# A two-layer attention kernel: pair sums formed behind the transposes, and half of an image's transposes kept in DRAM

## The chip, the cores and the metric

The kernel runs on one core of a Trainium2 chip. The time is device microseconds of one execution; the median of five runs before the change is 2765.83 us (2765.57 to 2766.76). Engines are named as the profile names them: PE (TensorE), DVE (VectorE), ACT (ScalarE), POOL (GpSimd), SP (SyncE, which only issues DMAs here). PEld is the loading of weights into PE.

## The reference, cut to what matters

The input x is 8 images of 256 channels and 96 x 96 pixels, float32. Two residual layers follow each other:

```python
x = x + layer0(group_norm(x))   # q, k, v = 1x1 convolutions, fft2 of each over (h, w)
                                # attention among the 32 channels of each of 8 heads
                                # out = abs(ifft2(attn @ v_f, axes=(-2, -1))) while out is (head, 32, 9216)
                                # then an output convolution
x = x + layer1(group_norm(x))   # linear attention with softplus features, 32 key channels
```

Layer 0 normalizes each row of the transformed q and k over all 9216 frequencies and takes softmax of the real and of the imaginary part of q k^T. The kernel computes no transform as such. q k^T over all frequencies needs only the covariance of x with x (for the norms) and of x with its mirrored image (pixel (h, w) beside pixel (-h, -w), modulo 96). With e = x + mirrored x and o = x - mirrored x both follow from e e^T and o o^T over half of the pixels; a pixel that is its own mirror gets the weight 1/sqrt(2). The inverse transform runs over the 32 channels and over the 9216 frequencies as one axis, so it does not undo the forward one: what is left of the two over the pixels is that each row of the image is multiplied by a 96 x 96 matrix that depends on the row (a window of a table). The code calls this rotating.

## The kernel before, in words

Channels lie on partitions: an image is [128, 2, 9216]. Two arenas in SBUF hold an image each; x of image b is in one, its rotated form y in the other, where x of image b+1 is loaded as soon as regions become free. Inside an arena the rows are permuted: tile t of 12 holds rows 4t to 4t+3 and then their mirrored rows (x_col, L102; tile 0 also holds rows 0 and 48). Tiles are worked from 11 down to 0.

For each image there are these stages, written as generators that yield between small pieces:

- `pair_sums(b)` (L323): 37 steps, 3 for each tile and one for the row that is left. `even_odd` (L296) makes e and o of a whole tile with one addition and one subtraction (L317; on Pool for most tiles, on VectorE for some, and a narrow column by Pool at L318), one tile or two ahead of their use. A step transposes a block of 128 pixels of e and of o on PE (L350, four transposes into one PSUM tile), ACT copies the result to a slot of `xT` (L353), and PE adds the products e e^T and o o^T (L331, eight matmuls; each float32 matmul appears as two in the profile). The products of a step are written after the transposes of the next one. VectorE takes the statistics of x for the group norm (L264).
- `attention(b)` (L367): group norm, then a chain of small matmuls and VectorE and ACT work that ends in the matrix `mz`.
- `rotate(b)` (L525): 48 steps of two rows. A step transposes two rows of x (L550, four transposes of 128 x 96), ACT copies them to a slot of `xT` (L563), and two steps later PE multiplies them with the row's window of the table (L553, eight matmuls in the profile), and VectorE copies the result into y (L558 for a column of sums, L559 for the pixels, backwards). `load_r` (L533) loads the windows of six rows into one of three `tm` buffers, from ACT's DMA queue (from SP's for image 0) in pieces of 384 bytes, and Pool fills one more column (L536).
- `images(b)` (L582): z = mz y (L621), squares and roots on ACT with additions on VectorE (L662) and Pool (L667), the output convolution (L633), the residual sum and the statistics for layer 1. x of image b+1 begins to be loaded.
- `layer1(b)` (L680): group norm, q and k (L718), softplus on VectorE and ACT, transposes of x (L779) copied out by ACT or VectorE (L782, L784), the products with k (L755).
- `output(b)` (L835): matmuls (L863), residual sums on VectorE (L868) and on Pool after an ACT copy (L871, L872), stores. The last tiles of x of image b+1 are loaded here.

The order of the work: `weave(stage, other)` (L884) runs a stage, and at each yield of n it takes n steps of the other one. `pair_sums(b + 1)` is woven into images, layer1 and output of image b; its last six steps follow alone (`finish`, L915). `rotate(b)` is woven into `attention(b)`; its last steps follow alone (L907). In attention the program's order holds on PE, in output on PE, DVE, Pool and SP; elsewhere a scheduler that plans with a cost model orders the instructions of each engine. [...] Buffers come from pools: `ring` has four buffers (e and o of a tile, the tiles of images, weights, scratch), `three` has three (`tm`), `psum` five banks.

## Time and profile before

| what | us |
|---|---|
| median of 5 runs | 2765.83 |
| the profiled execution | 2764.56 |
| its span, first to last instruction | 2762.7 |
| PE busy | 2720.2 |
| DVE busy | 1958.5 |
| ACT busy | 1367.6 |
| POOL busy | 843.5 |
| one image, from the last product of pair_sums to the same point of the next (412.82 to 752.64) | 339.8 |
| of it rotate with attention (412.8 to 490.6) | 77.8 |
| of it images (491 to 626), layer1 (626 to 680) and output with the last six steps (680 to 753) | 135, 54, 73 |
| transposes of rotate (L550), 1520 of them, busy on PE | 409.2 |
| matmuls of rotate (L553), 3040 of them, busy on PE | 472.7 |
| sums on Pool (L317), 136 of 128 x 760 | 246.0 |

In what follows a row of a group of instructions reads: line, engine, operation, output and input by name and shape, count, then busy time, mean nanoseconds of one, and the idle time of that engine ahead of them with what ended it. A row of the timeline reads: start, duration, engine, line, operation, count, and in brackets the idle time of the engine ahead of it with what ended it. A row of the waits reads: engine and line, what it waited for, total, times, longest. PE's instructions overlap, so that busy times of PE do not add up to elapsed time; the step from one instruction's start to the next does.

### The profile page before, as it was taken

Reading aid. Unit: us, or ns where it says so; the run is one execution under the profiler, and the core shown is the slowest. Engines: PE = TensorE matmul, PEld = TensorE weight load, DVE = VectorE, ACT = ScalarE, POOL = GpSimd, SP = SyncE. Lnnn points to the kernel's source line nnn. Section 1 sums busy time; section 2 is a strip of 40 time slices with the busy share of each in tenths; the row PEclk is TensorE's granted clock in tenths of the full one; section 3 lists DMA queues with packets and bytes.
Section 4 is the critical chain, followed back from the end, with each engine's and each line's share of the span. In section 5 each row is a group of like instructions: output and inputs, shape, how many; then the busy total and the mean of one; then the engine's idle time right before and its main releaser. Section 6 shows DMA issues by size and latency. Waiting matters only on the chain.

```text
span 2762.7 us, 47785 instructions
## 1 busy us (share of the span) xinstructions
PE 2720.2 (98%) x18348; PEld 1972.2 (71%) x18348; DVE 1958.5 (71%) x4104; ACT 1367.6 (50%) x2098; POOL 843.5 (31%) x939
## 2 busy tenths in 40 slices
PE   8999999999999999999999999999999999999988
PEld 8965679657795677956679567785678856788556
DVE  7588666876668767587675875769766687666776
ACT  3455634556345563354634546345453455544553
POOL 5034340342403423035230351313513135131311
PEclk9999999999999999999999999999999999999997
DMA  5120151201512015120151201521015210251003
GB/s 169 40 69 8 47 184 43 70 7 49 179 43 72 6 47 182 43 69 6 54 178 46 63 6 54 182 54 52 7 53 184 57 46 7 64 176 29 0 7 137
DMA packets 197273, 192.50 MB, mean 70 GB/s; under 512 B 88820, under 2 KB 197048, under 8 KB 197048
## 3 DMA queue, kind: packets, MB, share of 16 engines
q1 hardware_dynamic: 129800, 164.34, 18.5%
q10 hardware_dynamic: 67248, 25.12, 3.5%
q8 instruction: 146, 2.39, 0.4%
q14 instruction: 79, 0.65, 0.1%
HBM read 113.85 MB, written 75.57 MB: 69 GB/s over the span
## 4 chain that ended last, share of the span: by engine, by line
PE 93%; DVE 3%; ACT 2%; DMA 1%; issue 1%; POOL 1%; SPq 0%; POOLq 0%; DVEq 0%; ACTq 0%
PE z L621 20%; PE po L633 18%; PE acc L331 12%; PE y L553 10%; PE xr L550 6%; PE xT L779 5%; PE eoT L350 5%; PE kq L718 5%; PE o L863 4%; PE kx L755 3%; DMA arena<-in_x_dram 1%; PE cw L423 1%; PE kT L770 1%; DVE arena L559 1%; PE mz L511 1%
## 5 line engine op out<-in xcount | busy, mean ns | idle before, releaser
L621 PE MATMUL z<-arena,mz 128*128 128x384 f32 (+2 forms) x2400 | 595.0, 476 | 0.0
L633 PE MATMUL po<-e,wo 128*128 128x384 f32 x1536 | 529.7, 486 | 0.2 <-ACT e L668 0.2
L667 POOL TENSOR_TENSOR e<-e 128x768 f32<-128x768 f32 x192 | 348.1, 1815 | 554.1 <-ACT e L666 554.1
L621 PEld LDWEIGHTS z<-arena,mz 128*128 128x128 f32 (+1 forms) x2400 | 325.6, 163 | 241.4 <-issue 42.4
L553 PE MATMUL y<-tm,xT 96*128 96x97 f32 x3040 | 472.7, 261 | 1.7 <-ACT sd_a L288 0.5
L553 PEld LDWEIGHTS y<-tm,xT 96*128 96x128 f32 x3040 | 457.8, 192 | 12.5 <-issue 4.9
L331 PE MATMUL acc<-xT 128*128 128x256 f32 (+2 forms) x2368 | 439.8, 327 | 3.5 <-ACT xT L353 3.5
L633 PEld LDWEIGHTS po<-e,wo 128*128 128x128 f32 x1536 | 289.4, 190 | 197.7 <-DVE arena L635 1.2
L662 DVE TENSOR_TENSOR e<-z,xT 128x768 f32<-128x768 f32 x384 | 365.9, 953 | 85.2 <-PE z L621 85.1
L264 DVE BATCH_NORM_STATS2 st<-arena 128x6 f32<-128x384 f32 x768 | 406.7, 553 | 11.1 <-DMA arena<-in_x_dram 0.8
L550 PE MATMUL xr<-ident,arena 128*96 128x128 f32 x1520 | 409.2, 275 | 0.0
L331 PEld LDWEIGHTS acc<-xT 128*128 128x128 f32 (+1 forms) x2368 | 379.6, 191 | 37.6 <-ACT xT L353 5.2
L563 ACT COPY xT<-xr 96x512 f32<-96x512 f32 (+1 forms) x384 | 220.6, 578 | 293.5 <-PE xr L550 289.0
L666 ACT ACTIVATE e<-e 128x1536 f32<-128x1536 f32 x192 | 284.5, 1482 | 93.3 <-DVE e L662 91.8
L668 ACT ACTIVATE e<-e 128x768 f32<-128x768 f32 x192 | 162.0, 844 | 334.0 <-POOL e L667 332.9
L317 POOL TENSOR_TENSOR eo<-arena 128x760 f32<-128x760 f32 x136 | 246.0, 1809 | 252.3 <-issue 129.9
L635 DVE TENSOR_TENSOR arena<-arena,po 128x384 f32<-128x384 f32 x384 | 211.3, 552 | 94.4 <-PE po L633 70.5
L353 ACT ACTIVATE xT<-eoT 128x512 f32<-128x512 f32 x280 | 166.8, 598 | 183.2 <-PE eoT L350 181.6
L550 PEld LDWEIGHTS xr<-ident,arena 128*96 128x96 f32 x1520 | 227.2, 150 | 10.3 <-issue 6.9
L559 DVE COPY arena<-y 128x384 f32<-128x384 f32 (+1 forms) x384 | 209.9, 547 | 1.2 <-issue 0.5
L558 DVE COPY ys<-y 128x4 f32<-128x4 f32 (+1 forms) x384 | 62.5, 163 | 199.1 <-PE y L553 195.7
L350 PE MATMUL eoT<-ident,eo 128*128 128x128 f32 (+1 forms) x1184 | 189.0, 280 | 11.8 <-POOL eo L318 11.8
(202 smaller groups left out, 2912.6 us busy)
## 6 DMA issues: line engine op xcount, KB each, us to landing
arena<-in_x_dram SPq DMA_DIRECT2D x184, 384.0 KB
out_dram<-arena SPq DMA_DIRECT2D x184, 384.0 KB
tm<-rt ACTq DMA_DIRECT2D x112, 216.0 KB
tm<-rt SPq DMA_DIRECT2D x16, 216.0 KB
arena<-in_x_dram SPq DMA_DIRECT2D x8, 288.0 KB
out_dram<-arena SPq DMA_DIRECT2D x8, 288.0 KB
wl<-in_w1t_dram SPq DMA_DIRECT2D x8, 256.0 KB
wl<-in_w2t_dram SPq DMA_DIRECT2D x8, 256.0 KB
```

Of the source, the lines that this page charges most:

```text
L264: nc.vector.bn_stats(out=st[:, k, c, :], in_=x_of(b)[:, k, c * CH:(c + 1) * CH])
L317: op(d[:, :, lo:hi, 1:W], x_t[:, :, ra:ra + n, 1:W], x_t[:, :, back, W - 1:0:-1])
L331: mm = nc.tensor.matmul(acc[c][:, m * C:m * C + (KC - m) * P], lhsT=t[0:np_, c, m * P:(m + 1) * P], rhs=t[0:np_, c, m * P:C], start=(first ...
L350: nc.tensor.transpose(pt[0:np_, c * C + k * P:c * C + (k + 1) * P], eo[:, c, k, i:i + np_], ident)
L550: nc.tensor.transpose(pt[0:W, r * C + k * P:r * C + (k + 1) * P], x_of(b)[:, k, o:o + W], ident)
L553: nc.tensor.matmul(pu[:, o:o + W + 1], lhsT=gt[0:W, r, k * P:(k + 1) * P], rhs=tm[:, g % TR + r, :], start=True, stop=True)
L559: nc.vector.tensor_copy(y[:, :, :, g + r:g + 2], src[:, :, W - 1::-1, r:2])
L621: mm = nc.tensor.matmul(out[:, o:o + n * W], lhsT=columns(mz, k, c, j), rhs=y[:, k, h * W:(h + n) * W], start=(k == 0 and o == 0), stop=(k ...
L633: nc.tensor.matmul(po[:, 0:CH], lhsT=wo[:, k, m * P:(m + 1) * P], rhs=e[:, k, :], start=(k == 0), stop=(k == KC - 1))
L662: nc.vector.tensor_add(e[:, 2 * c:2 * c + 2, :].rearrange("p t (q h) -> p t q h", h=H), pz[:, 0:CH].rearrange("p (q h) -> p q h", h=H).uns ...
L666: nc.scalar.activation(e, e, AF.Square)
L667: nc.gpsimd.tensor_add(e[:, 0:2, :], e[:, 0:2, :], e[:, 2:4, :])
```

## The change

1. **e and o are made after the transposes.** `even_odd` goes. A step of `pair_sums` now transposes a block of x itself and a mirrored copy of its partners (`back`, two buffers), again four transposes into one PSUM tile. ACT copies both to SBUF with a weight for each pixel (`pw`, a column for each kind of step: 0 for a pixel that would count twice, 1/sqrt(2) for one that is its own mirror), and then e and o are formed of the two in a slot of `xT`: by Pool from SBUF (two operations of 256 columns), or by VectorE from PSUM and SBUF. In later images Pool does it for tiles 9 to 11 and for all but the first step of tiles 0 to 5, VectorE for the rest; in image 0 they alternate. The mirrored copy is made one step ahead by Pool, by ACT for tiles 0 to 5 of later images. Column 0 of the image goes through a small tile `w0`, filled by Pool; the last two steps of an image, which mix pieces of rows 0, 48 and `w0`, need 8 and 9 small copies.
2. **Half of the transposes are kept in DRAM.** In images 1 to 7 the steps of tiles 6 to 11 also store the transposed x and the transposed mirrored copy to `xtd` in DRAM (two DMAs of 128 KB a step from SP), and two transposes of `w0` supply column 0. In `rotate` the rows 24 to 71 except 48 and 49 are then loaded from there three steps ahead (`fetch`, 192 KB for a step, SP), in place of four transposes and an ACT copy. Rows that come from the mirrored copy are stored the other way round, so their table windows come from a second table `rb`.
3. **The order of rotate** alternates between three steps of one kind and three of the other (`pieces`). The windows of the table are put together once, stored to `rx` in DRAM and read back from there as one block by later images; all these DMAs are issued from SP.
4. **Smaller shifts.** Three yields in attention become longer (3, 5, 3 to 4, 8, 4); the weights `wl` are loaded at the second step of tile 0 instead of at the start of attention; two buffers for layer 1 are taken at the start of images; in layer 1 half of VectorE's copies of transposed x go to ACT.

The diff, cut to its core:

```diff
+        def turn_back(i):
+            t, j = steps[i]
...
+            front = ab[0][2] if ready else xts[-1][:, j % 3, 0].rearrange("p (k n) -> p k n", k=KC)
+            for p0, n, *v in ab:
+                for c in range(ready, 2):
+                    if v[c] is not None:
+                        (nc.scalar.copy if b and t < T0 else nc.gpsimd.tensor_copy)(
+                            (front, back[:, i % 2])[c][:, :, p0:p0 + n], v[c])
+            return front, xts[-1][:, j % 3]
...
+        for i, (t, j) in enumerate(steps):
+            front, both = ahead
+            if i + 1 < len(steps):
+                ahead = turn_back(i + 1)
+            pt = ps_tile(f"eoT_{b}_{t}_{j}").rearrange("p (c n) -> p c n", c=2)
+            for k in range(KC):
+                nc.tensor.transpose(pt[:, 0, k * P:(k + 1) * P], front[:, k], ident)
+                nc.tensor.transpose(pt[:, 1, k * P:(k + 1) * P], back[:, i % 2, k], ident)
+            nc.scalar.activation(both, pt, AF.Copy, scale=pw[:, j:j + 1])
+            if b and t >= T0:
+                n = P - j // 2
                 for c in range(2):
...
+                    nc.sync.dma_start(out=turned(c, PR * t, 1 + P * j)[0:n], in_=both[0:n, c])
+            eo = sum_slot()[:, :, 0:C]
+            if (j if t < T0 else t > NT - 4) if b else j % 2:
+                nc.gpsimd.tensor_add(eo[:, 0], both[:, 0], both[:, 1])
+                nc.gpsimd.tensor_sub(eo[:, 1], both[:, 0], both[:, 1])
+            else:
+                for c, op in enumerate((ALU.add, ALU.subtract)):
+                    nc.vector.scalar_tensor_tensor(eo[:, c], in0=pt[:, 0], scalar=pw[:, j:j + 1], in1=both[:, 1],
+                                                   op0=ALU.mult, op1=op)
+            if pending is not None:
+                products(*pending, first, False)
...
-        yield 3
+        yield 4
...
-            yield (5, 3)[m]
+            yield (8, 4)[m]
...
+            turned = H // 2 <= h < H - PR * T0
+            if b > turned:
+                nc.sync.dma_start(out=tm, in_=rx[h // TR])
+                return tm
...
+        pieces = [TR * i for i in (15, 4, 0, 5, 14, 6, 1, 8, 13, 7, 2, 9, 12, 10, 3, 11)]
+        order = [h + r for h in pieces for r in range(0, TR, 2)]
...
+        def fetch(i):
+            if i < len(order) and spilled(order[i]):
+                xts[i] = xT[:, i % NX]
+                h = order[i]
+                c = h > H // 2
+                rows = turned(c, H - h - 1 if c else h, 0)[0:2 * W]
+                nc.sync.dma_start(out=xts[i][0:W, :, 0:C], in_=rows.rearrange("(r w) n -> w r n", w=W))
...
+            step(None if spilled(h) else h, pending.pop(0) if len(pending) == 2 else None, xts[i])
+            pending.append((h, xts.pop(i), tm))
+            fetch(i + 3)
...
-                    if jj or i % 3 == 2:
+                    if jj or i % 6 > 1:
                         nc.scalar.copy(xt[jj][:, :, 0:C], src)
```

## The prediction

> **What bounds the kernel.** I read the page first, busy time and then the chain that ended last; after it the waits of PE alone, and the timeline wherever the change touches the order of work.

> ```profile
> PE 2720.2 (98%) x18348; PEld 1972.2 (71%) x18348; DVE 1958.5 (71%) x4104; ACT 1367.6 (50%) x2098; POOL 843.5 (31%) x939
> PE 93%; DVE 3%; ACT 2%; DMA 1%; issue 1%; POOL 1%; SPq 0%; POOLq 0%; DVEq 0%; ACTq 0%
> PE z L621 20%; PE po L633 18%; PE acc L331 12%; PE y L553 10%; PE xr L550 6%; PE xT L779 5%; PE eoT L350 5%; PE kq L718 5%; PE o L863 4%; PE kx L755 3%; DMA arena<-in_x_dram 1%; PE cw L423 1%; PE kT L770 1%; DVE arena L559 1%; PE mz L511 1%
> ```

> PE is on the chain for 93% of the span, in every stage. A busy PE need not be a fast one, so I asked what PE itself ever waits for:

> ```profile
> PE eoT L350 <- POOL eo L318: 11.8, 21, 7.0
> PE kT L770 <- DVE arena L748: 3.6, 1, 3.6
> PE acc L331 <- ACT xT L353: 3.5, 7, 0.5
> ```

> The whole list comes to about 32 us in 2762.7 (columns: total, times, longest). So PE work that is taken away shortens the span, and every wait that is added to PE lengthens it.

> **What goes.** Of the 48 steps of rotate in an image, the pairs of rows from 24 to 70 except 48 lose their four transposes (L550): 23 steps in each of images 1 to 7, 161 steps, 644 of 1520 transposes. The price of one step is in the trace, since the last steps of rotate already run without transposes. The start of the small copy (L558) marks the steps:

> ```profile
> 823.08 0.16 DVE L558 COPY ys<-y 128x4 f32<-128x4 f32 x1 [0.61 <-PE y L553]
> ...
> 824.31 0.17 DVE L558 COPY ys<-y 128x4 f32<-128x4 f32 x1 [0.61 <-PE y L553]
> ...
> 827.67 0.16 DVE L558 COPY ys<-y 128x4 f32<-128x4 f32 x1 [0.27 <-PE y L553]
> ...
> 828.57 0.17 DVE L558 COPY ys<-y 128x4 f32<-128x4 f32 x1 [0.27 <-PE y L553]
> ```

> A mixed step takes 1.235 us (821.84 to 824.31 is two), a step without transposes 0.895 us (826.78 to 828.57 is two), and VectorE still waits 0.27 us for PE in it. Saved: 161 x 0.34 = 55 us. The chain of waits puts a transpose at 0.11 us, which would make 161 x 0.44 = 71 us; but those two steps are free of gaps on PE and nevertheless take 0.11 us for each of 8 matmuls, against 0.10 us for each of the 12 in the mixed step, so I take 55. The small end: VectorE has 0.71 us of copies in a step (L558 and L559) and is busy for 11.26 of the 15 us from 445 to 460, where the softmax lies. If some 8 spilled steps of an image gain nothing there, 7 x 8 x 0.34 = 19 us are lost and 36 remain.

> [...]

> **What is added to PE directly.** Two small transposes of w0 in each later image: 14 x 0.11 = +1.5 us. The 37 x 4 transposes and 37 x 8 products of pair_sums stay as many.

> **The new path of a sum.** Before, Pool or VectorE had made e and o a whole tile ahead, and a product waited for ACT alone. Now it waits for transposes, then ACT, then the sum:

> ```profile
> 743.57 0.60 ACT L353 ACTIVATE xT<-eoT 128x512 f32<-128x512 f32 x1 [1.15 <-PE eoT L350]
> ...
> 744.95 1.39 PEld L331 LDWEIGHTS acc<-xT 128*128 128x128 f32 x8
> ...
> 745.42 1.42 DVE L317 TENSOR_TENSOR eo<-arena 128x570 f32<-128x570 f32 x2 [0.80 <-DMA arena<-in_x_dram]
> ```

> ACT ended at 744.17, its products start at 744.95: 0.78 us of slack for c=0, and 0.65 us more (four of the eight products, 1.31 us) for c=1. ACT now takes a scale per partition: the form with half takes 689 ns, not 598, so 0.69 us of slack remain. A sum of 256 columns on Pool lies between L318 (8 columns, 0.21 us when undisturbed) and L872 (384 columns, 1.004 us); with L667 (768, 1.815 us) the slope is 2.1 ns a column, so 0.735 us. On VectorE L830 (256 columns, one operand in PSUM) takes 0.381 us. So a VectorE step is covered; a Pool step is late by 0.05 us for c=0 and, with 0.735 us more, 0.1 us for c=1 plus semaphores. In output PE has 0.98 us of o matmuls in each step besides, and in the kq stage 5.3 us: covered. Uncovered are three places.

> (a) The six steps after output. Pool and SP keep the program's order there. The copies for (0,0), among them four w0 copies on Pool, are written ahead of the sum of (1,2), and all need the last tile of x, which lands at 745.42 (the row above, VectorE waiting for it). ACT's order is the scheduler's. Then come 8 and 9 small copies on ACT for the last two steps. Their bounds are L726 (1 column, 0.203 us) and L405 (128 columns, 0.263 us), so about 0.23 us each, 4 us together, against 1.75 us of PE (0.44 + 1.31) a step and 0.69 us of ACT. Followed through by hand the last product ends about 2 us later than now, less if ACT puts its ready work first: 1.5 us an image, +10.5 us, ends 0 and 3.5 us an image (0 and +24).

> (b) Around layer1's group norm three steps stand almost alone on PE (629 to 635). Pool then makes for each step two sums, a mirrored copy (L224, 48 columns, 0.218 us, and L530, 192 columns, 0.524 us, give 0.66 us for 256) and a third of the w0 copies: 1.47 + 0.66 + 0.22 = 2.35 us against 1.75. That is 0.6 us x 3 if nothing was made ahead: +1 us an image, +7 us, ends 0 and +14.

> (c) In the kx stage (645 to 680) ACT is busy for 27.08 of 35 us and gets 6 copies more (L782, 0.59 us) and 0.09 us per step: 31.4 of 35. I take +0.5 us an image, +3.5 us, ends 0 and +7.

> The trace shows Pool held up by VectorE: at 734.30 two L318 took 1.80 us while two L317 ran, elsewhere 0.21 us each. [...]

> [...]

> **Waits whose cover shrinks.** In the attention the matmul of qkm (L392) waits for the reciprocal of the deviation:

> ```profile
> 759.44 0.15 DVE L379 TENSOR_TENSOR dmm<-mv_a,rstd_a 128x2 f32<-128x2 f32 x1
> ...
> 759.72 0.53 PEld L392 LDWEIGHTS qkm<-wl,dmm 128*2 128x2 f32 x8
> ```

> The slack is 0.13 us. The two steps ahead of it become spilled ones, shorter by 0.68 us: +0.55 us, +3.9 us for seven images. Elsewhere the longer yields (4, 8, 4 for 3, 5, 3) give as much cover as before: 8 steps of about 1.05 us against 5 of 1.235.

> The spilled loads: ACT's 23 copies (L563) go, a load of 192 KB comes in their place, issued after step i for a step whose matmuls run five steps later, at least 4.4 us. The nearest row is the load of tmat, 0.73 to 4.15 us, 3.4 us with the start of the program in it: hidden with 1 us to spare. SP took 0.47 us to issue a quiet weight load (L371), under 0.89. The tm loads move from ACT's queue to SP behind the out stores, which land by 750.95 (Pool's L530 waits for them); the first tm is needed at 756.4. The 36 large stores an image (128 KB each) fall into 626 to 680, where the DMA share is 0.19 at most, not into 715 to 753, where it is 0.87 to 0.91. All at nothing.

> **Image 0** has no spill. Its sums on VectorE stand in order behind tables(), about 6 us of VectorE work (L233 to L253) that an e and o made ahead used to hide; on the other side the first step needs a 0.66 us copy where PE waited 7.0 us for Pool. Ends -3 and +6, I take +2.5.

> **Sum**, against the profiled execution's 2764.56 us (span 2762.7): -55 + 1.5 + 10.5 + 7 + 3.5 + 3.9 + 2.5 = -26.6. The median is 1.3 us above the profiled time: 2765.8 - 26.6 = 2739.

> **Rivals.** *Cover holds everywhere*: -55 + 1.5 = 2712. For it speaks that the waits in (a) to (c) are each under 4 us and ACT is at 50%; against it the slack of 0.05 us. Chance 0.15. *The sums become the path*: if a product waits for both sums, a Pool step needs 0.09 + 0.69 + 1.47 + 0.1 = 2.35 us against 1.75, 0.6 us late in 8 steps of each later image and 13 of image 0 (41 us), with 14 us for the small copies: -55 + 1.5 + 3.9 + 41 + 14 + 3.5 + 2.5 = +11, 2777. It turns the sign once a later image loses 7.1 us ((55 - 1.5 - 3.9) / 7). Against it: the products of c=0 come first. Chance 0.13. *Spilled steps stay as long*: if a load costs SP what it does in output, where 16 issues took 19.65 us (1.23 us each), a spilled step stays near 1.235: no saving, +25, 2791. Against it the DMA share of 0.16 in rotate. Chance 0.05. *The costs eat the gain*, at the upper ends of (a) to (c) and image 0: -55 + 1.5 + 24 + 14 + 7 + 3.9 + 6 = +1, 2767. Chance 0.10. The forecast keeps 0.57.

> **Numbers.** A measurement of this kernel tells 0.2% (5.5 us) from no change. Faster: 0.57 + 0.15 = 0.72; within: 0.10; slower: 0.13 + 0.05 = 0.18. The forecast's own range is 2714 to 2760; the one given, 2706 to 2772, takes in full cover and the eaten gain, and leaves out most of the 0.18 and a little below.

> **What would show it.** L550's successor with 876 transposes and 14 for w0; spilled steps 0.89 us apart by the small copy; PE's waits naming Pool's sums only around group norm and after output, under 4 us an image. Wrong if products wait for Pool or VectorE in most steps, if y waits for a DMA, or if the spilled steps are paced by VectorE.

## The result, and the profile after

The changed kernel takes 2772.23 us (median of 22 runs, 2764.69 to 2784.29), the kernel before on the same chips 2765.74 (41 runs): a ratio of 1.0025, interval 1.0018 to 1.0031. The change costs 0.25%, where the forecast was a gain of 27 us. The profiled execution took 2775.92 us with a span of 2774.1. It is 11.4 us longer than the span before; the medians differ by 6.5 us. The times now scatter by 20 us where they scattered by 10, and this execution lies in the upper half; why they scatter is a part of the answer.

The page's first line and the waits of PE (total, times, longest), to be read beside those of before:

```profile
PE 2693.2 (97%) x17718; PEld 1941.8 (70%) x17718; DVE 1967.7 (71%) x4237; ACT 1372.5 (49%) x2230; POOL 848.9 (31%) x1199
```

```profile
PE acc L329 <- POOL xT L406: 22.6, 24, 3.3
PE acc L329 <- DVE xT L410: 11.0, 7, 1.6
PE qkm L459 <- issue: 7.7, 7, 1.1
PE eoT L398 <- POOL back L383: 4.7, 3, 2.2
PE eoT L397 <- DMA arena<-in_x_dram: 4.6, 1, 4.6
```

PE is busy for 27 us less (2693.2 for 2720.2), and waits in three places where it did not: products for Pool's sums, products for VectorE's sums, once an image, and qkm (the last two rows belong to image 0). The chain of waits is no help here: it can be followed only through the last 70 us.

The spilled steps are what the forecast said, 0.89 to 0.90 us apart (VectorE's timeline, start and duration; before 1.235):

```profile
767.80 0.16 DVE L657 COPY ys<-y 128x4 f32<-128x4 f32 x1 [0.35 <-PE y L652]
767.88 0.55 DVE L658 COPY arena<-y 128x384 f32<-128x384 f32 x1
768.70 0.17 DVE L657 COPY ys<-y 128x4 f32<-128x4 f32 x1 [0.27 <-PE y L652]
```

So I cut both traces at the same instructions and compared stage by stage. "Tail" is from the end of the last o product to the last product of the sums, and "rotate" from there to the first matmul of the next stage; us, summed over the seven times that each occurs.

| stage | before | after | difference |
|---|---|---|---|
| image 0, start to last product | 74.7 | 80.8 | +6.1 |
| rotate of images 1 to 7 | 514.7 | 476.7 | -38.0 |
| images 0 to 6 | 1021.7 | 1022.0 | +0.3 |
| layer1, images 0 to 6 | 513.4 | 529.7 | +16.3 |
| output, images 0 to 6 | 229.9 | 225.5 | -4.4 |
| tails | 101.3 | 131.3 | +30.0 |
| last image behind its rotate | | | +1.1 |

Two rows hold what was not foreseen. A tail takes 17.3 to 19.9 us (before 14.1 to 14.8). And rotate takes 66.7 or 66.8 us in four images, 6.8 less than before, but 69.9 or 70.0 in three. The windows of the trace say why (stretch; busy us of PE, PEld, DVE, ACT, POOL with counts; granted clock, DMA share, GB/s):

```profile
1089.90:1093.30 3.40, 1.16 (x6) 1.09 (x7) 0.00 (x0) 1.85 (x7) 1.92 (x6) 1.00 1.05 363
1093.30:1096.70 3.40, 3.40 (x14) 2.92 (x13) 1.03 (x3) 2.58 (x11) 1.93 (x3) 0.51 0.71 234
...
1106.90:1110.40 3.50, 2.40 (x23) 2.21 (x23) 2.52 (x11) 2.13 (x3) 0.00 (x0) 1.00 0.10 16
1110.40:1113.80 3.40, 3.40 (x17) 2.13 (x14) 1.17 (x4) 0.00 (x0) 0.00 (x0) 0.50 0.18 54
1113.80:1117.20 3.40, 3.40 (x19) 3.40 (x19) 3.06 (x10) 0.64 (x2) 0.00 (x0) 0.50 0.21 61
```

A stretch of 3.4 us in which PE stood idle for 2.2 us (the tail) or 1.1 us (ahead of qkm) is followed by one or two stretches at half the granted clock. There are 11 halved stretches between images 1 and 7, five in tails and six in rotate, and none before the change. Half speed for 3.41 us loses up to 1.7 us: up to 8.5 us in the tails, and 3 x 3.2 = 9.7 us in rotate (69.9 against 66.7).

### The profile page after: what moved, and what is told of

It is laid out like the page before. It is cut to its first block, busy times and chain, and to the rows that moved or that the text cites. A ratio compares the mean times of both kernels' runs of the same rounds, so it can differ in the third digit from the quotient of the medians.

```text
span 2774.1 us, 47811 instructions
## 1 busy us (share of the span) xinstructions
PE 2693.2 (97%) x17718; PEld 1941.8 (70%) x17718; DVE 1967.7 (71%) x4237; ACT 1372.5 (49%) x2230; POOL 848.9 (31%) x1199
## 5 line engine op out<-in xcount | busy, mean ns | idle before, releaser
L740 PE MATMUL po<-e,wo 128*128 128x384 f32 x1536 | 529.7, 486 | 0.2 <-ACT e L775 0.2
L329 PE MATMUL acc<-xT 128*128 128x256 f32 (+1 forms) x2368 | 454.7, 334 | 33.6 <-POOL xT L406 22.6
L329 PEld LDWEIGHTS acc<-xT 128*128 128x128 f32 x2368 | 386.7, 193 | 80.3 <-POOL xT L406 27.9
L652 PE MATMUL y<-tm,xT 96*128 96x97 f32 x3040 | 430.4, 270 | 4.9 <-ACT xT L661 3.6
L652 PEld LDWEIGHTS y<-tm,xT 96*128 96x128 f32 x3040 | 419.2, 195 | 16.7 <-issue 8.5
L399 ACT ACTIVATE xt<-eoT,pw 128x512 f32<-128x512 f32 x296 | 202.6, 687 | 165.2 <-PE eoT L398 161.5
L661 ACT COPY xT<-xr 96x512 f32<-96x512 f32 (+1 forms) x223 | 127.3, 575 | 281.1 <-PE xr L649 281.1
L649 PE MATMUL xr<-ident,arena 128*96 128x128 f32 x876 | 231.5, 278 | 0.0
L410 DVE SCALAR_TENSOR_TENSOR xT<-eoT,pw,xt 128x256 f32<-128x256 f32 x258 | 112.2, 477 | 114.1 <-ACT xt L399 98.5
L971 DVE TENSOR_TENSOR arena<-arena,o 128x384 f32<-128x384 f32 x288 | 142.1, 550 | 35.9 <-PE o L966 35.7
L383 POOL COPY back<-arena 128x256 f32<-128x256 f32 (+1 forms) x167 | 72.6, 441 | 302.9 <-PE eoT L398 302.7
```

What stands on the lines that cost most here:

```text
L329: mm = nc.tensor.matmul(acc[c][:, m * C:m * C + (KC - m) * P], lhsT=t[0:np_, c, m * P:(m + 1) * P], rhs=t[0:np_, c, m * P:C], start=(first ...
L399: nc.scalar.activation(both, pt, AF.Copy, scale=pw[:, j:j + 1])
L649: nc.tensor.transpose(pt[0:W, r * C + k * P:r * C + (k + 1) * P], x_of(b)[:, k, o:o + W], ident)
L652: nc.tensor.matmul(pu[:, o:o + W + 1], lhsT=gt[0:W, 1 - r if back else r, k * P:(k + 1) * P], rhs=tm[:, g % TR + r, :], start=True, stop=True)
L740: nc.tensor.matmul(po[:, 0:CH], lhsT=wo[:, k, m * P:(m + 1) * P], rhs=e[:, k, :], start=(k == 0), stop=(k == KC - 1))
```

## Theories

- **O, order.** In the tail, copies that need the last tile of x stand in ACT's and Pool's queues ahead of work that is due. PE runs dry, and the idle PE then gets half the clock.
- **D, transfers.** The added DMAs make x's last tile land later.
- **S, thin stream.** Rotate now feeds PE so thinly that its clock is halved, whatever the waits do.

For O speaks the timeline of a tail of the changed kernel:

```profile
1088.59 0.27 PE L398 MATMUL eoT<-ident,back 128*128 128x128 f32 x1
1090.38 0.24 ACT L383 COPY xt<-arena 128x64 f32<-128x64 f32 x1 [3.99 <-DMA arena<-in_x_dram]
...
1090.53 0.68 ACT L399 ACTIVATE xt<-eoT,pw 128x512 f32<-128x512 f32 x1
...
1091.36 0.72 POOL L406 TENSOR_TENSOR xT<-xt 128x256 f32<-128x256 f32 x1 [4.82 <-ACT xt L399]
...
1092.14 1.85 PE L329 MATMUL acc<-xT 128*128 128x256 f32 x8 [3.27 <-POOL xT L406]
```

PE finished the transposes of step (1,1) at 1088.86. ACT could have taken them then; but a copy of 64 columns for step (0,2), four steps later, stands ahead of it and waits for x until 1090.38. ACT, Pool's sum and PE's product follow in a row.

## The experiments

All are compared with the kernel before; the ratio is given with its interval.

### One cause each

**e1_tail**: ACT too keeps the program's order in output, and the copies for (0,0) are written behind the sum of (1,2).

```diff
+            late = b and (t, j) == (1, 2)
-            if i + 1 < len(steps):
+            if i + 1 < len(steps) and not late:
...
+            if late:
+                ahead = turn_back(i + 1)
...
-        with tc.manual_schedule(engines={mybir.EngineType.PE, mybir.EngineType.DVE, mybir.EngineType.Pool, mybir.EngineType.SP}):
+        with tc.manual_schedule(engines={mybir.EngineType.PE, mybir.EngineType.DVE, mybir.EngineType.Pool, mybir.EngineType.SP,
+                                         mybir.EngineType.Activation}):
```

> Edit to the changed kernel: in output ACT too keeps the program's order, and the copies for the first step of tile 0 are written after the activation and the sum of the step before. Theory O (order): in the changed kernel a copy out of the last tile of x stands ahead of the activation of step (1,1) in ACT's queue, PE idles 1.7 to 3.3 us for it, and where that idle fills much of a 3.4 us stretch the granted clock is halved in the next one. Then the wait of the products for Pool in the last six steps falls under 0.5 us, the time from the last matmul of output to the last product from 17.4 to 19.9 us down to about 15, the five halved stretches in these places go, those in rotate (after the wait of qkm) stay: 7 x 2.5 + 5 x 1.7 = 26 us less, about 2746. Rival D (DMA): the last tile of x lands too late because of the added DMA traffic, the order does not matter: the wait moves to the transposes of (0,0) and the time stays at 2772. Rival S (thin stream): the clock is halved because rotate keeps PE less dense: the same ten or so halved stretches, about 2755.

Measured: 2755.9 us, 0.997 (0.9958 to 0.9982). The tails fall from 131.3 to 117.6 us. That is less than O expected, because two new waits came with the same order: 16 small copies now stand in a row ahead of the activations of the last two steps, and Pool's copy of a column of y waits 3.1 us for an output store ahead of a sum. The time is the one S named, but not for its reason: rotate takes 66.7 or 66.8 us in six of seven images, with its stream as thin as ever.

**e2_yield3**: one more step of rotate ahead of qkm, to cover VectorE's chain.

```diff
-        yield 2
+        yield 3
         pb = ps_tile(f"qkm_{b}")
```

> Edit to the changed kernel: one more step of rotate ahead of the matmul of qkm (yield 3 for 2). Theory O: PE's 1.1 us wait there goes (7.7 us in all), and with it the three pairs of halved stretches early in rotate, 3 x 3.3 us; rotate takes 66 us in each of images 1 to 7; the tail stays as it is: about 17 us less, 2755. Rival S (the clock is halved because rotate without half of its transposes is a thinner stream): only the 7.7 us go, the halved stretches in rotate stay, 2764. Rival D expects what O does here.

Measured: 2756.11 us, 0.9971 (0.9962 to 0.998). Rotate takes 65.9 or 66.0 us in six images and 66.7 in one, with no halved stretch in it. O holds, S does not: the stream of those steps is the same. The tails stay at 129.3 us.

**e4_fill**: 24 transposes of the identity into a spare bank, ahead of the product that waits in the tail.

```diff
+            if b and (t, j) == (1, 2):
+                idle = ps_tile(f"idle_{b}")
+                for k in range(24):
+                    nc.tensor.transpose(idle[:, k % 4 * P:(k % 4 + 1) * P], ident, ident)
```

> Edit to the changed kernel: 24 transposes of the identity that nothing reads are put on PE after the transposes of step (1,2) of images 1 to 7, 24 x 0.11 = 2.6 us, where PE idles 1.7 to 3.3 us now. Theory O: the wait is filled, not shortened, so that the halved stretches of the tail go (5 x 1.7 = 8.5 us) while 2.6 us stand in place of 1.7 or 3.3 of idle: between 2762 and 2770, and the clock record shows halved stretches in rotate alone. Rival S, and any theory in which idle time of PE is not what halves the clock: as many halved stretches as before, and 2774 to 2778.

Measured: 2764.89 us, 1.0011 (0.9996 to 1.0027). Work for nothing, and the kernel is 7 us faster than the changed one: the profiled execution has no halved stretch before the last image, neither in the tails nor behind qkm. That execution is the fastest of ten, though. Two others took 2776.54 and 2780.57 us at a mean clock of 0.987 and 0.985, so half clock came there too, at places that no trace shows; the wait ahead of qkm stayed open in this edit.

**e11_fill_qkm**: the same with 12 transposes in the wait ahead of qkm.

```diff
         pb = ps_tile(f"qkm_{b}")
+        if b:
+            idle = ps_tile(f"idle_{b}")
+            for k in range(12):
+                nc.tensor.transpose(idle[:, k % 4 * P:(k % 4 + 1) * P], ident, ident)
```

> Twelve transposes of the identity into a spare PSUM bank ahead of qkm's first matmul in images 1 to 7: work for nothing in the 1.1 us for which PE waits there. They take 1.3 us at full clock, so the wait is filled and 0.2 us an image is added. Theory (an idle PE halves the clock of the next stretches): no halved stretch behind qkm, rotate 66.9 us in every image where three of seven had 69.9: 2772 + 1.5 - 10 = 2760 to 2766. Rival (the thin stream of weight loads in rotate halves it, or the tail's waits alone): halved stretches behind qkm stay, 2773 to 2776.

Measured: 2763.51 us, 0.9992 (0.9983 to 1.0001). Rotate takes 66.9 us in all seven images; three halved stretches remain in the tails. So here it is the idle time that brings the half clock, and the 1.1 us ahead of qkm do not cost 1.1 us but up to 4.3 (with 69.9 for 66.7 us of rotate).

**e7_yield1** goes the other way, a step less ahead of qkm and a longer wait.

```diff
-        yield 2
+        yield 1
         pb = ps_tile(f"qkm_{b}")
```

> One step of rotate instead of two ahead of the matmul of qkm: the wait there grows from 1.1 to about 2.0 us, PE's work stays the same. Theory O with the clock: 0.9 us more of waiting in each of seven images is 6 us, and the longer idle stretch is followed by halved clock in most images, 3.3 us each time: 2782 to 2795, five or more of the seven later images with a halved stretch right after qkm. Rival (what halves the clock has nothing to do with the length of this wait): 6 us alone, 2776 to 2780, halved stretches after qkm in three of seven as now.

Measured: 2789.59 us, 1.0086 (1.0071 to 1.0101). The wait grows only to 1.4 us, and yet rotate takes 71.7 us in five of seven images and 66.8 in two. Windows of this kernel at image 1:

```profile
430.20:433.60 3.40, 1.96 (x19) 1.46 (x19) 2.34 (x10) 2.13 (x3) 0.00 (x0) 1.00 0.00 0
433.60:437.10 3.50, 3.50 (x18) 2.96 (x15) 1.69 (x5) 0.27 (x1) 0.00 (x0) 0.51 0.00 0
437.10:440.50 3.40, 3.40 (x16) 3.14 (x16) 2.83 (x10) 0.37 (x1) 0.00 (x0) 0.50 0.44 124
440.50:443.90 3.40, 3.40 (x14) 2.49 (x13) 0.98 (x2) 0.02 (x1) 0.00 (x0) 0.50 0.22 63
```

1.4 us of idle in one stretch, then three stretches at half clock: 5 us. Rotate's sum is 492.1 us against 476.7, which is nearly the whole loss of 17 us against the changed kernel.

**e6_start**: Pool keeps the program's order in the sums of image 0, where column copies that wait for a load had been put ahead of the mirrored copies.

```diff
-    with tc.manual_schedule(engines={mybir.EngineType.DVE}):
+    with tc.manual_schedule(engines={mybir.EngineType.DVE, mybir.EngineType.Pool}):
```

> Edit to the changed kernel: in the sums of image 0 Pool keeps the program's order too. Theory O: image 0 ends its last product at 80.8 us, 6 us later than before the change, since Pool stands with w0 copies that wait for a later tile of x while PE waits 4.7 us for the mirrored copies behind them; with the program's order these waits go and the last product is at 75 or 76: 5 us less, 2767, nothing else changes but the phase of the clock's stretches (plus or minus 5 us). Rival: image 0 is late because of the new path (transposes, ACT, sum) and of tables() on VectorE, not of Pool's order: the last product stays at 80 us, 2772.

Measured: 2771.13 us, 1.0021 (1.0009 to 1.0033): nothing won, as the rival said. The wait of 2.2 us ahead of 10.68 is gone, but a sum on Pool now waits 2.0 us behind VectorE's tables (L267), mirrored copies stand behind the sum, PE waits 1.76 us until 34.55, and a halved stretch follows at 35.0. Image 0 ends at 80.8 us as before the edit.

**e3_tail_yield**: e1 and e2 together.

> Both edits at once: ScalarE keeps the program's order in the output stage, with the mirrored copy of step (0,0) written behind the sum of (1,2), and three steps of rotate instead of two ahead of the matmul of qkm. Alone they gave -16 us each against the changed kernel. Theory O (a product or the qkm matmul that waits in an in-order queue, and then a halved clock in the stretch after the wait): the two waits lie 30 us apart in each image and each has its own halved stretches, so the gains add up: 2738 to 2746 us, tails of 16 to 17 us, rotate 65.9 in every image, at most one halved stretch before the last image. Rival (both edits cure one and the same thing, the clock of the same stretches): the gains overlap, 2752 to 2756.

Measured: 2748.08 us, 0.9935 (0.992 to 0.9949), 2 us above what O gave. Rotate 66.0 in every image, tails 117.3 us, no halved stretch before the last image. The two gains of 16 us add up to 24: they cure some of the same halved stretches, for e1 alone had left only one of three in rotate.

### Where the gain of the spill went

**e5_nospill**: no store of transposes, no fetch; every step transposes its own rows, all else is the changed kernel.

```diff
-            if b and t >= T0:
+            if False:
...
-            if b and (t, j) == (T0, 2):
+            if False:
...
-            return b > 0 and PR * T0 <= h < H - PR * T0 and h != H // 2
+            return False
```

> The spill alone is taken back: no stores of transposes to DRAM, no fetches, every step of rotate transposes its own two rows again; the new path of the sums and the yields stay as in the changed kernel. Theory O: rotate goes back from 66.7 to 73.5 us less the covered qkm wait (0.7 us), tails stay at 17 to 20 us since they come from the order of ScalarE's and Pool's copies; so about 2772 + 7 x 6.5 = 2810 to 2822 us, i.e. the sums' new path costs 45 to 55 us against the kernel before by itself. Theory D (stores and fetches make the last tile of x land late): tails fall to 15 to 16 us, x lands 4.3 us after the last o as before, 2795 to 2805.

Measured: 2794.0 us, 1.01 (1.0083 to 1.0117), below both expectations. Against the changed kernel the spill is worth 22 us, not 50. The tails give the reason: 114.6 us instead of 131.3, though the order of ACT's copies is the same. So D has a part in it. SP's timeline in the changed kernel shows the place (start, duration of the issues):

```profile
704.20 7.25 SPq L403 DMA_DIRECT2D xtd<-xt  x6
716.93 5.62 SPq L431 DMA_DIRECT2D xtd<-xt  x2
722.61 0.34 SPq L635 DMA_DIRECT2D xT<-xtd  x1
722.99 2.61 SPq L985 DMA_DIRECT2D out_dram<-arena  x4
725.65 2.37 SPq L139 DMA_DIRECT2D arena<-in_x_dram  x2
728.13 16.98 SPq L985 DMA_DIRECT2D out_dram<-arena  x16
745.21 2.66 SPq L139 DMA_DIRECT2D arena<-in_x_dram  x3
```

The two small stores of w0's transposes (L431) each wait some 5 us for the store ahead of them to land (the row of SP's waits below). In output SP issues in the program's order, and the first output store stands behind them: it leaves at 722.99, 8.4 us after the first o product at 714.61. Before the change it left at 713.91, 5.6 us after the first o product at 708.29 (the other two rows), and without the spill it is 5.3 us.

```profile
SPq L431 <- DMA xtd<-xt: 71.9, 14, 5.4
```

```profile
713.91 2.57 SPq L882 DMA_DIRECT2D out_dram<-arena  x4
716.57 2.76 SPq L135 DMA_DIRECT2D arena<-in_x_dram  x2
```

From 722.99 on the DMA share of the changed kernel soon stands at 1.04 to 1.08 (730 to 755), nothing is caught up, and ACT's copy that waits for x starts 4.1 to 5.6 us after the last o product; without the spill the same copy starts 2.5 to 3.6 us after it.

**e10_defer**: the two stores eight steps later, with step (3,2).

```diff
             if b and (t, j) == (T0, 2):
-                n = H // 2 - PR * T0
                 pt = ps_tile(f"w0T_{b}")
...
                 nc.scalar.copy(col[0:H + 1 - PR * T0], pt[0:H + 1 - PR * T0, 0:C])
+            if b and (t, j) == (T0 - 3, 2):
+                n = H // 2 - PR * T0
                 for c in range(2):
```

> The two small stores of w0's transposes to DRAM are issued eight steps later (with step (3,2) instead of (6,2)); nothing else differs from the changed kernel. There SyncE waits 5 us for an earlier store at that place, the first fetch is queued behind it, and the first output store leaves 8.4 us after the first o product (before the change 5.6, without the spill 5.2); the transfers of x's last tile then land 4.1 to 5.6 us after the last o product instead of 2.5. Theory D (SyncE's queue makes x late, and the order of ScalarE's copies turns that into PE's wait): output stores start 2.5 us earlier, tails fall from 17.4-19.9 to about 16.5, no halved clock there: 2755 to 2762. Theory O alone (the order of the copies is all): x lands when it did, 2768 to 2776.

Measured: 2783.9 us, 1.0054 (1.0035 to 1.0073), against both expectations. The output stores do start earlier, 5.3 us after the first o product, but the stall has only moved: SP stands for some 4 us in the middle of them, the DMA share falls to 0.80 from 730 to 740, the last loads of x leave 0.1 to 1.3 us ahead of the end of the o products instead of 1.4 to 2.1, and the tails take up to 22.3 us.

**e14_last**: the two stores behind all output stores and loads of x, with step (0,1).

```diff
-            if b and (t, j) == (T0 - 3, 2):
+            if b and (t, j) == (0, 1):
```

> The two small stores of w0's transposes are issued behind all output stores and all loads of x (with step (0,1)); nothing else differs from the changed kernel. With step (3,2) the stall of SyncE had only moved: the last loads of x were issued still later (1.2 us ahead of the end of the last o product, against 1.6 in the changed kernel and 2.3 without the spill) and the tails grew with them. Theory D (the tails follow the issue of x's last loads on SyncE): now nothing stalls SyncE between the stores, the last loads of x go 2.3 us or more ahead, tails 16 to 17 us in every image and no halved clock in them: 2752 to 2762, unless the first spilled step then waits for its fetch, which would show as y waiting for a DMA. Theory O alone: tails of 17.4 to 19.9 stay, 2768 to 2776.

Measured: 2753.64 us, 0.9957 (0.9943 to 0.9971): D. SP's timeline now:

```profile
717.89 2.58 SPq L986 DMA_DIRECT2D out_dram<-arena  x4
720.56 2.75 SPq L139 DMA_DIRECT2D arena<-in_x_dram  x2
723.41 19.08 SPq L986 DMA_DIRECT2D out_dram<-arena  x16
742.58 3.28 SPq L139 DMA_DIRECT2D arena<-in_x_dram  x3
...
752.07 0.79 SPq L432 DMA_DIRECT2D xtd<-xt  x2
```

The first output store leaves 5.3 us after the first o product (712.6), the tails take 114.4 us, as without the spill, and the edit of two small DMAs is worth 18.6 us. The order of the copies is untouched here, and in e1 the stores are: each edit alone brings the tails to 114 to 118 us, so late transfers and the order of the copies made them long together.

### The waits taken away together

**e9_best**: the edits of e1, e2 and e6; half of the small copies of the last two steps on Pool instead of ACT; the column of y written behind all sums; one of the two steps behind layer1's bias moved ahead of it; VectorE's tables of image 0 cut in four, with two steps between each.

```diff
-                        (nc.scalar.copy if b and t < T0 else nc.gpsimd.tensor_copy)(
+                        (nc.scalar.copy if b and t < T0 and not (c and t == 0 and j > 1) else nc.gpsimd.tensor_copy)(
...
+        yield 1
         zero = own[:, 5 * C:5 * C + 1]
...
         nc.vector.tensor_add(bvs, bvs, pv[:, 0:C])
-        yield 2
+        yield 1
...
-        tables()
+        for _ in tables():
+            next(sums)
+            next(sums)
```

> All waits that the traces name, taken away together: ScalarE in the program's order in output and the mirrored copy of (0,0) late; the small copies that end in the back half of the last two tiles' steps on Pool, those of the front half on ScalarE; the column copy of y written behind all sums; three steps ahead of qkm; one of the two steps behind layer1's bias moved ahead of it; Pool in the program's order in the sums of image 0, and VectorE's tables there cut in four with two steps between each. Theory O: 2742 as for the two edits together, less 7 x 0.8 in the tails, 7 x 1.2 in layer1 and 4 at the start: 2720 to 2730 us, no halved stretch before the last image. Rival (the time comes from elsewhere than these waits): 2738 or more.

Measured: 2727.8 us, 0.9863 (0.9848 to 0.9878), as O expected. Tails 104.5 us, rotate 462.2, layer1 524.9, image 0 ends at 76.9.

**e12_best_defer**: e9 with the stores of e10.

> The version without the named waits, and with the late stores of w0's transposes besides. There products wait for Pool for 3 us in all by now and the tails take 14.7 to 15.3 us, so an earlier landing of x has little left to shorten: by theory O 2724 to 2729 against 2728; if x's landing still sets the tails, 2720 to 2724.

Measured: 2729.11 us, 0.9865 (0.9849 to 0.9881). The moved stall shows again (one tail of 18.7 us and one of 16.5).

**e15_best_last**: e9 with the stores of e14.

> The version without the named waits, with the small stores of w0's transposes behind all output stores. Its tails take 14.7 to 15.3 us, 0.3 to 0.9 us more than before the change, and products wait for Pool for 3 us in all: by theory O nothing is left to win, 2725 to 2730; by theory D it is safer against late transfers and wins at most 7 x 0.4 us: 2722 to 2727. If the first spilled steps wait for their fetch, 2730 to 2740.

Measured: 2722.82 us, 0.9845 (0.983 to 0.986), the fastest version, 43 us below the kernel before. Its waits of PE, to be read beside those of the changed kernel:

```profile
PE eoT L401 <- DMA arena<-in_x_dram: 4.6, 1, 4.6
PE kT L884 <- DVE arena L866: 3.6, 1, 3.6
PE xT L893 <- ACT xT L896: 3.4, 7, 0.5
PE qkm L466 <- PE y L662: 3.1, 7, 0.4
PE y L662 <- ACT xT L671: 2.9, 7, 0.4
PE acc L332 <- POOL xT L410: 2.9, 14, 0.4
```

The products' wait for Pool has gone from 22.6 to 2.9 us and that for VectorE is off the list. Of the 5 us against e9, the profiled executions show 1 us between image 0's last product and image 7's (2346.0 for 2347.0) and 4.5 in the last image, where half clock held for 13 us this once, against 46 in e9. The other three executions had the usual clock in the mean and the same time; where they gain is open.

**e13_best_nospill**: e9 with the three lines of e5, that is, without the spill.

> The version without the named waits, and without the spill: no stores of transposes, no fetches, every step of rotate with its own transposes. If the saving of the spill was sized rightly in the prediction (55 us less 1.5 for w0's transposes) and the rest of the loss was waits, this takes 2728 + 50 = 2774 to 2782 us; if the spill is worth only what taking it back from the changed kernel cost (22 us), 2748 to 2755.

Measured: 2772.64 us, 1.0022 (1.0013 to 1.0032). Once the waits are gone, the spill is worth 44.8 us (49.8 against e15, whose small stores no longer hold SP up). Rotate takes 512.0 us without it and 462.2 with it: 0.31 us for each of the 161 steps. The sums' new path alone, even with its waits mended, is 6 us slower than the old one.

## Why the prediction was wrong

| step of the prediction | us predicted | us shown | by |
|---|---|---|---|
| 161 spilled steps at 0.34 | -55 | -49.8 | rotate, e13 to e9 |
| w0's transposes, and what else the spill adds in layer1 | +1.5 | +1.2 and +2.4 | layer1, e5 to after and e13 to e9 |
| (a) six steps after output | +10.5 | +13.1 | tails, before to e14 |
| (b) around layer1's group norm | +7 | +0.3 | images, before to after |
| (c) layer1's kx stage | +3.5 | +11.9, w0's transposes in it | layer1 and output, before to after |
| qkm | +3.9 | +5, and 9.7 of half clock | rotate, e2 to after |
| image 0 | +2.5 | +6.1 | before to after |
| stores and fetches on SP | 0 | +16.9, up to 8.5 of it half clock | tails, e14 to after |

The column of what was shown comes to +13 (w0's transposes counted once), the spans differ by 11.4.

**The step that failed** is the one that ended "All at nothing". It counted the 36 large stores, put them into 626 to 680, and priced the issue of a transfer. It did not count the two small stores, nor ask what each store on SP waits for and what is queued behind it. In the changed kernel stores of transposes are issued until 711, and the two small ones hold SP until 722.6, in front of the output stores and the loads of x. They cost 16.9 us in the profiled executions (tails of 131.3 and 114.4) and 18.6 in the medians.

**The other failure is a price, the same for all waits**: a wait of PE was put at its own length. The prediction never asked what clock PE would have behind it. Half clock cost up to some 18 us of the profiled execution. It fits that the times scatter: over the 22 executions they rise as the mean clock falls (2764.69 us at 0.990, 2784.29 at 0.984), and the ten executions of e13, without a halved stretch before the last image in its trace, lie within 1.6 us.

Length alone does not decide what follows a wait. All halved stretches of a trace lie on one grid of 3.41 us, and laid over the waits of the changed kernel it shows what does (it runs through 1093.35, where the first halved stretch begins, in steps of 3.4133 us: the last passage at half clock begins at 2765.88, 490 steps on):

| image | 1 | 2 | 3 | 4 | 5 | 6 | 7 |
|---|---|---|---|---|---|---|---|
| longest wait in the tail, us | 2.03 | 1.73 | 3.27 | 2.43 | 2.80 | 2.15 | 2.76 |
| most of it in one stretch of the grid, us | 1.48 | 1.11 | 2.20 | 2.10 | 2.22 | 2.08 | 1.98 |
| half clock behind the tail | no | no | yes | yes | yes | yes | yes |
| the wait of 1.1 us ahead of qkm ends, us into its stretch | 0.62 | 0.69 | 3.26 | 1.17 | 3.28 | 0.99 | 3.14 |
| half clock behind qkm | no | no | yes | no | yes | no | yes |

The other traces agree. In the tails of all fifteen with the new path, the 24 waits of which 1.92 us or more fell into one stretch were all followed by half clock. Of the other 81 tails one was (e1, where two waits of 0.75 and 0.92 us shared a stretch); a wait of 3.27 us in e2, which the grid cuts into 1.75 and 1.52, was not. Ahead of qkm, six traces have the wait of 1.1 us in seven images each: the 10 of these 42 that were followed by half clock ended in the last 0.3 us of a stretch or 0.03 us after it, the other 32 elsewhere. In e7, with 1.4 us, the five with half clock behind them ended 2.6 to 2.8 us into a stretch, the other two at 0.7 and 1.0. So a wait costs its own length, and half clock besides where the grid cuts it badly. No halved stretch in the tail is needed for one behind qkm (e1 and e14 have one without), and why 1.1 us are enough there, but not in a tail, is open.

**Right in kind**: the spill's gain, 0.31 for 0.34 us a step; fetches that come in time, for PE never waits for one; (a), once SP's stall is taken out, 1.9 us an image for 1.5; Pool's sum, 0.73 us where the slope gave 0.735; the activation with a scale, 687 ns for 689; sums covered in output. Products wait for Pool in 24 steps of 296, so the rival in which the sums become the path did not happen, though its 2777 us lies 5 us from the time. So does the 2767 us of the rival in which the costs eat the gain, which is right in kind, but by luck: the largest costs, SP and the half clock, are not among those that it adds up. Pool's mirrored copies were held up beside VectorE, as L318 was before the change (two in 1.80 us, elsewhere 0.21 us each): 21 of the 161 copies of 256 columns, three in each later image, took 0.77 to 0.84 us with a VectorE instruction of two SBUF inputs beside them (L852, L854, L855), the other 140 took 0.39 or 0.40 us, 68 alone and 72 beside other instructions of VectorE. It cost PE no wait: its waits for a mirrored copy lie in image 0 alone.

**qkm**: of the cover, 0.6 us went as predicted. The rest of the 1.1 us is that the chain itself grew by 0.5 us, on VectorE. The root on ACT starts 1.90 us after the matmul that it waits for, before and after. But VectorE takes two copies of a spilled step first (from 768.70), and its reciprocal starts 0.59 us after the end of the root, where it was 0.04 us (three rows after the change, two before):

```profile
768.39 0.26 ACT L311 ACTIVATE sd_a<-gv_a,epsb 128x2 f32<-128x2 f32 x1
768.78 0.55 DVE L658 COPY arena<-y 128x384 f32<-128x384 f32 x1
769.24 0.16 DVE L313 RECIPROCAL rstd_a<-sd_a 128x2 f32<-128x2 f32 x1
```

```profile
758.87 0.26 ACT L288 ACTIVATE sd_a<-gv_a,epsb 128x2 f32<-128x2 f32 x1
759.17 0.17 DVE L290 RECIPROCAL rstd_a<-sd_a 128x2 f32<-128x2 f32 x1
```

The prediction took the chain as fixed.

**(b) and (c)**: around the group norm nothing is lost. The loss is at a place the prediction didn't name, just behind layer1's bias: ACT's table load and two logarithms come first in its queue, the activations of two steps behind them, and PE waits 1.57 us for VectorE's sum, once in each of seven images (11.0 us in all, where it waited 0.5 us for ACT before, 3.5 in all). ACT and PE there:

```profile
660.21 1.28 ACT L853 ACT_TABLE_LOAD   x1
661.50 1.12 ACT L853 ACTIVATE spu<-spu,own 128x384 f32<-128x384 f32 x2
662.53 1.24 ACT L399 ACTIVATE xt<-eoT,pw 128x512 f32<-128x512 f32 x2
```

```profile
664.13 1.58 PE L329 MATMUL acc<-xT 128*128 128x256 f32 x8 [1.57 <-DVE xT L410]
```

In e9, with one step ahead of the bias, this wait goes; 3.4 us of waits for ACT come in its place, and layer1 gains 4.8 us in all. No run places the rest of the loss in layer1. Of the 4.4 us by which output became shorter about half is the cut between the stages: before, two products with `rec` started behind the first o product in each image (708.52 after 708.29), and now they run ahead of it. The other half is open.

**Image 0**: around the tables PE waits once, for 1.1 us. More lies in the first 16 us: mirrored copies stand behind Pool's column copies, which wait for loads, PE waits for them for 1.4 and 2.2 us, and its transposes stay 0.21 us apart until 11.4 and its products slow until 15.6, where 0.11 us is usual; before the change that pace is reached by about 11 us. The record of the granted clock agrees: its first entry, at full clock, begins at 14.74 us, before the change at 10.28. With Pool in order and the tables cut, e9 gets 3.9 of the 6.1 us back.

## What to carry to other kernels

When DMAs are put on a queue, write down for each what it waits for and what stands behind it; two small stores that wait 5 us each in front of the output stores cost 18.6 us here, more than the sums' new path with its waits mended (6 us). When a change thins the cover of PE, price a wait at its length plus the half clock that can follow it, here up to 3.2 us behind a wait of 1.1 us. And test a trade of work for waits without the waits before it is given up: here 49 us (2772.2 to 2722.8) lay behind edits of the order and of which engine makes a small copy.

## What the runs showed of the hardware

A mirrored copy of 256 columns on Pool took 0.40 us alone, 0.77 to 0.84 us beside a VectorE instruction of two SBUF inputs (L852, L854, L855) and 449 ns in the mean, where the prediction had 0.66. Small ACT copies that stand in a row start 0.13 to 0.15 us apart, where it had 0.23.
